# A four-layer image kernel: DVE's product with C one state later, a meter for layer 1's taps, and tiles that rest behind their stores

## The chip, the cores and the metric

The kernel runs on one core of a Trainium2 chip. The metric is the device time of one execution in microseconds. The engines are named as in the profile: PE is TensorE (PEld its weight loads), DVE is VectorE, ACT is ScalarE, POOL is GpSimd, and SP is SyncE, whose queue issues nearly all DMAs of the main part. Each engine works through its own instructions in the order in which the program was written.

## The reference

Four images of 384 channels and 48 x 48 pixels (2304 tokens) pass through four layers. Each layer normalises over groups of channels (`_gn`) and adds its result to its input.

```python
# layer 0, for each image, over 2304 tokens in order (d = 768 channels, s = 16 states)
xin, z = split(gn(x) @ in_proj.T)
xin = silu(causal_depthwise_conv4(xin))
dt, B, C = split(xin @ x_proj.T); dt = softplus(dt @ dt_proj.T + b)
h = exp(dt * A) * h + dt * B * xin        # a scan for each channel and state
y = sum_s(h * C) + xin * D                # the product with C, added over the states
x = x + layer_norm((y * silu(z)) @ out_proj.T)
# layer 1: 1x1 conv, a filter on 8x8 patches in the Fourier domain, a 3x3 depthwise
#          conv (9 taps), gelu(first half) * second half, 1x1 conv
# layer 2: an 11x11 depthwise conv
# layer 3: 4 experts (two 384x384 products with relu), weighted by a top-2 router
```

## The kernel before

**Layer 0 and its slots.** An image is cut into five chunks of 460 or 464 tokens (`CHUNKS`). A chunk has 96 steps, called slots here: 6 blocks of 128 channels times 16 states. So there are 4 x 5 x 96 = 1920 slots (`N`), and `scans` writes the program out slot by slot, in the order in which each engine is to run it. For state `u`, `decay(u)` (line 942, ACT) writes exp(dt A) to a PSUM bank `da`; `drive(u)` (line 953, POOL) writes `bu`, the input times B; `scan(u)` (line 966, DVE) runs the recurrence; the product with C gives `g`; and `turned` (line 886, PE) transposes and adds `g` into `y`. The product runs on POOL in slow slots (`product`, line 995; then the scan writes to `g` in SBUF) and on DVE in the others (`product_now`, line 986; then the scan writes over `da`). In image 0 one slot in three is slow, later every second one. `keep` (line 980, ACT) copies the scan's last column to `carry` for the next chunk; in a slot that is not slow it comes after the product.

There are three banks for `da` in image 0 (the bank for `acc` serves as the third) and two later. Decays are issued three slots ahead in image 0, two ahead later. `bu` has three buffers, `g` six. B and C of a pair of slots come from HBM, broadcast to all partitions, by `spread` (line 930), which issues on SP.

**Everything else.** All other work is cut into tasks, which are Python generators. Each `yield` names a kind of step: "act", "pe", "dve" and "late" (DVE work after the product), "pool", with a weight, a ring of buffers that it needs, and a condition. A task takes at most one step a slot. `Lane.step` goes through the active tasks, and a step runs if its ring has a free buffer. A step with a weight also needs the meter: it counts PE work by weight, falls by 2.3 a slot, takes 0.44 for the slot's own adds, and admits up to 3.7. Steps on DVE have no weight and are not limited, with one exception: layer 1's nine taps of a block (`taps` in `finish_strip`, lines 1413 and 1415) go in threes in slots with `place % 4 < 2`, in twos in the others.

The lanes are `aux` (the rest of layer 0: projections, gates, output projection, layer norm, residual), `start` (during image 0: statistics and z projections of images 2 and 3, kept in HBM), `one` (layers 1, 2 and 3's router of the image before, in this order, begun 42 slots into an image) and `two` (the experts: for each image 4 experts times 16 strips of 144 tokens, 64 blocks). A block loads a strip of x3d (and from the second expert on the partial sum y3d), runs two products on PE (line 1750), adds on DVE (line 1782, or 1785 for the first expert) and stores. What the scans have not taken of image 2's work follows in the tail with image 3's layers; the experts of image 3 end it (`all_experts`, lines 1850 and 1867).

**Rings.** `Ring` counts the buffers of a tile in the planner. A buffer counts as free once `done` was called for it, which for a stored tile is right behind the issue of the store. The hardware still makes the next load into it wait until the store has landed; that wait stands in SP's queue.

Of the kernel before, what the change touches and what calls it, by code (L numbers as in the profile page):

```python
# [16 lines left out]
P = 128  # L17
# [11 lines left out]
NE = 4  # L29
# [13 lines left out]

class Ring:


    def __init__(self, make, n):
        self.make, self.n, self.read = make, n, []

    def free(self, k=1):  # L50
        return all(self.read[: max(0, len(self.read) + k - self.n)])
# [6 lines left out]
    def done(self, k):  # L58
        self.read[k] = True


class Meter:


    def __init__(self, each, limit):
        self.each, self.limit, self.value = each, limit, 0.0

    def slot(self, given):
        self.value = max(0.0, self.value - self.each) + given
# [25 lines left out]
class Lane:  # L95
# [7 lines left out]
    def step(self, phase, slot, at=0):  # L103
        for task in self.active:
            if task.ended:
                continue
            kind, weight, ring, when = task.next
            if PHASE.get(kind, 1) != phase or task.after > slot:
                continue
            if weight and self.bound and self.meter.value + weight > self.meter.limit:  # L110
                continue
            if (ring and not ring[0].free(ring[1])) or (when and not when()):
                continue
            self.meter.value += weight
            task.move(slot)
        self.active = [t for t in self.active if not t.ended]
        while (
            self.queue and len(self.active) < self.width and self.queue[0].at <= max(at, slot)
            and all(t.ended for t in self.queue[0].needs)
        ):  # L120
            task = self.queue.pop(0)
            task.move()
            if not task.ended:
                self.active.append(task)

    def drain(self, slot, others=()):
        n = 0
        while self.queue or self.active:
            self.meter.value = 0.0
            for phase in range(3):  # L130
                for lane in (self, *others):
                    lane.step(phase, slot + n, 1 << 30)
            n += 1
            assert n < 20000, "stuck"
# [8 lines left out]
def tile_layers(ctx: ExitStack, tc: tile.TileContext, a: dict, out: bass.AP):  # L143
# [22 lines left out]
    gexp = const("gexp", [GROUPS, C], a["c_gexp"])  # L166
# [8 lines left out]
    def group_norm(st, bank, mean, rstd, name):  # L175

        mv = small.tile([P, CT, 2], F32, name=f"mv{name}", tag="mv")
        for ct in range(CT):
            nc.vector.bn_aggr(mv[:, ct, :], st[:, ct].rearrange("p k s -> p (k s)"))

        def to_groups(src, n, what):
            ps = bank(f"g{what}{name}")
            for ct in range(CT):
                nc.tensor.matmul(
                    ps[:GROUPS, :n], lhsT=gsel[:, ct, :], rhs=src(ct),
                    start=ct == 0, stop=ct == CT - 1,
                )
            return ps[:GROUPS, :n]

        def to_channels(src, n, what):  # L190
            ps = bank(f"c{what}{name}")
            for ct in range(CT):
                nc.tensor.matmul(
                    ps[:, n * ct : n * ct + n], lhsT=gexp[:, bass.ts(ct, P)], rhs=src,
                    start=True, stop=True,
                )
            return ps[:, : n * CT]

        grp = small.tile([GROUPS, 2], F32, name=f"grp{name}", tag="grp")
        nc.vector.tensor_copy(grp, to_groups(lambda ct: mv[:, ct, :], 2, "m"))  # L200
        nc.vector.tensor_copy(mean, to_channels(grp[:, 0:1], 1, "m"))
        dev = small.tile([P, CT], F32, name=f"dev{name}", tag="dev")
        nc.vector.tensor_sub(dev, mv[:, :, 0], mean)
        nc.vector.tensor_mul(dev, dev, dev)
        var = small.tile([GROUPS, 1], F32, name=f"var{name}", tag="var")
        nc.vector.scalar_tensor_tensor(
            var, to_groups(lambda ct: dev[:, ct : ct + 1], 1, "v"), GN_EPS, grp[:, 1:2],
            ALU.add, ALU.add,
        )
        nc.gpsimd.tensor_tensor(var, var, neghalf[:GROUPS, 0:1], ALU.pow)  # L210
        nc.vector.tensor_copy(rstd, to_channels(var, 1, "v"))

    def group_norm_steps(st, ring, mean, rstd, name):
# [15 lines left out]
        def to_channels(src, n, what):  # L229
            ps, k = ring.take(f"c{what}{name}")  # L230
            for ct in range(CT):
                nc.tensor.matmul(
                    ps[:, n * ct : n * ct + n], lhsT=gexp[:, bass.ts(ct, P)], rhs=src,
                    start=True, stop=True,
                )
            return ps[:, : n * CT], k
# [179 lines left out]
    with ExitStack() as first:  # L416
# [55 lines left out]
        stats0 = wp.tile([P, 2, CT, 2, 3, 6], F32, name="stats0")  # L472
# [86 lines left out]
        def scans(wk, mm, ring, meter, place, lanes, begin):  # L559
# [9 lines left out]
            def image_stats(b, ct, h):  # L569
# [4 lines left out]
                for k in range(3):  # L574
                    yield ("dve",)
                    nc.vector.bn_stats(stats0[:, b % 2, ct, h, k, :], t[:, bass.ts(k, LB)])

            def image_norm(b):
                yield from group_norm_steps(
                    stats0[:, b % 2].rearrange("p c h k s -> p c (h k) s"), ring,  # L580
# [4 lines left out]
            def early_stats(b, ct, h):  # L585
# [6 lines left out]
                for k3 in range(3):  # L592
                    yield ("dve",)
# [9 lines left out]
            def early_fold(b):  # L603
# [21 lines left out]
                yield ("dve",)  # L625
# [11 lines left out]
            def early_z(b, t, j):  # L637
# [22 lines left out]
                yield ("pool",)  # L660
# [28 lines left out]
            def fold(b, which):  # L689
# [22 lines left out]
                yield ("dve",)  # L712
# [25 lines left out]
            def project(i, j):  # L738
# [27 lines left out]
                yield ("dve",)  # L766
# [74 lines left out]
            def steps(i, p):  # L841
# [22 lines left out]
                yield ("dve",)  # L864
# [146 lines left out]
            def gate(i, m):  # L1011
# [9 lines left out]
                yield ("late",)  # L1021
# [4 lines left out]
            def out_proj(i, k):  # L1026
# [20 lines left out]
                yield ("dve",)  # L1047
# [4 lines left out]
            def layer_norm(i):  # L1052
# [8 lines left out]
                yield ("dve",)  # L1061
# [12 lines left out]
            def residual(i, ct):  # L1074
# [14 lines left out]
                yield ("dve",)  # L1089
# [86 lines left out]
            for tag, shape, n in (  # L1176
# [7 lines left out]
                    n,  # L1184
# [14 lines left out]
            with tc.manual_schedule():  # L1199
# [10 lines left out]
                for u in range(N + 6):  # L1210
# [17 lines left out]
                    meter.slot(0.44)  # L1228
                    soon = u % PAIR >= 8
# [5 lines left out]
                    if u < N:  # L1235
# [3 lines left out]
                    if decays < N and decays <= u + (3 if decays < LEN * NC else 2):  # L1239
# [15 lines left out]
                while aux.queue or aux.active:  # L1255
                    at += 1
                    meter.slot(0.0)
                    for phase in range(3):
# [5 lines left out]

        def slow_slot():
            return place[0] % 4 < 2

        def later(b, ring, accr):
# [11 lines left out]
            def slots(tag, shape, n):  # L1280

                return Ring(
                    lambda name: d["wk"].tile(shape, F32, name=name, tag=tag, bufs=n), n
# [11 lines left out]
            def begin1():  # L1295
# [3 lines left out]
                w = d["w_out"] = wk.tile([P, 2, C], F32, name=f"w_out1_{b}", tag="w_out", bufs=1)  # L1299
                nc.sync.dma_start(w[:, 0, :], a["L1_w_outT"][:P, :])  # L1300
                nc.sync.dma_start(w[64:P, 1, :], a["L1_w_outT"][P:, :])
# [38 lines left out]
            def patches(hb, wb):  # L1340
# [24 lines left out]
                yield ("late",)  # L1365
# [27 lines left out]
            def finish_strip(hb):  # L1393
# [7 lines left out]
                def taps(ct):  # L1401
# [3 lines left out]
                    room = 3 if slow_slot() else 2  # L1405
                    for k in range(9):
                        if not room:
                            yield ("dve",)
                            room = 3 if slow_slot() else 2
                        room -= 1  # L1410
# [18 lines left out]
                yield ("dve",)  # L1429
# [6 lines left out]
                yield ("dve",)  # L1436
# [3 lines left out]
                for ct in range(CT):  # L1440
# [3 lines left out]
                        ps[:, :LB], lhsT=w[:, 0, bass.ts(ct, P)], rhs=act[:, 0, :],  # L1444
# [3 lines left out]
                        ps[:, :LB], lhsT=w[64:P, 1, bass.ts(ct, P)], rhs=act[64:P, 1, :],  # L1448
                        start=False, stop=True,
                    )  # L1450
                    yield ("late",)
# [26 lines left out]
            xbs = slots("xb", [P, max(BANDS) * W], 2)  # L1478
# [68 lines left out]
            def windows(ct, k, r, first, last, final):  # L1547
# [26 lines left out]
                if last:  # L1574
                    yield ("late",)
# [5 lines left out]
                    yield ("pool",)  # L1581
# [40 lines left out]
            xg = slots("xg", [P, CT, LB], 2)  # L1622

            def begin3():
# [16 lines left out]
                yield ("dve",)  # L1641
# [4 lines left out]
            def scores_of(hb):  # L1646
# [23 lines left out]
                yield ("dve",)  # L1670
# [17 lines left out]
        def experts(b, ring, rings):  # L1688
# [15 lines left out]
            def begin(e):  # L1704
# [21 lines left out]
                yield ("late",)  # L1726
# [4 lines left out]
            def load3(s, e):  # L1731
                yield (
                    "pool", 0, None,
                    lambda: rings["xe"].free() and (not e or rings["ye"].free()),
                )
                x = take(("x", s, e), "xe", f"xe{b}_{s}_{e}")
                nc.sync.dma_start(x, strip(x3d[b], bass.ts(s, EB)))
                if e:
                    y = take(("y", s, e), "ye", f"ye{b}_{s}_{e}")
                    nc.sync.dma_start(y, strip(y3d, bass.ts(s, EB)))  # L1740
                yield from wait(3)

            def block(s, e):
# [33 lines left out]
                yield ("late",)  # L1777
                key = ("y" if e else "x", s, e)
                x = d[key][0]
                if e:  # L1780
                    y = x.rearrange("p c t -> p (c t)")
                    nc.vector.tensor_add(y, ps[:, : CT * EB], y)  # L1782
                else:
                    for m in range(CT):
                        nc.vector.scalar_tensor_tensor(
                            x[:, m, :], ps[:, bass.ts(m, EB)], b2_sum[:, m : m + 1],
                            x[:, m, :], ALU.add, ALU.add,
                        )
                ring.done(r)
                yield ("pool",)  # L1790
                nc.sync.dma_start(strip(out[b] if e == NE - 1 else y3d, bass.ts(s, EB)), x)
                done(key)
# [106 lines left out]
        def of_experts(pool, sizes):  # L1899
            for tag, n in sizes.items():  # L1900
# [5 lines left out]
                    n,  # L1906
# [11 lines left out]
        meter = Meter(2.3, 3.7)  # L1918
        one, two = Lane(8, meter), Lane(4, meter)

        def begin(b):
# [10 lines left out]
            {"we": 1, "xe": 2, "ye": 2, "hr": 1},  # L1932
        )
        with (
# [7 lines left out]
            while not all(ring.read):  # L1942
# [6 lines left out]
        with (  # L1949
# [4 lines left out]
            of_experts(wk, {"we": 2, "xe": 3, "ye": 3, "hr": 3})  # L1954

            one.queue += later(NB - 1, ring, accr)
            while one.queue or one.active or two.queue or two.active:
                at += 1
                meter.slot(0.0)
                if not (one.queue or one.active):  # L1960
# [124 lines left out]
```

## Time and profile before

| | |
|---|---|
| median of 3 runs | 5400.23 us (5399.6 to 5402.55) |
| the profiled execution | 5405.14 us, span 5403.1 us |
| busy over the span | PE 86%, DVE 75%, POOL 62%, ACT 55% |
| image 0 (480 slots) | 86 to 1047 us |
| images 1, 2, 3 | to 2161, 3344 and 4516 us |
| tail | to 5403 us |
| a scan on DVE | 1.17 us, 1920 times |
| a product with C on DVE, on POOL | 0.63 us, 1035 times; 1.16 us, 885 times |
| a decay on ACT, a `bu` on POOL | 0.65 us, 1.17 us, 1920 times each |
| taps on DVE (line 1415) | 0.615 us, 576 times |
| PE work of the experts in lane `two` | 485.0 + 484.7 us for 192 blocks |

The times of images are those of the first scan of each, counted from the span's start. An engine's busy share is an average over stages in which different engines are scarce, so each stage is read by itself. A row of waits names the instruction that stood idle, and what released it.

### The profile page before, as it was taken

The page shows a single profiled execution, that of the slowest core. Times are in us where ns is not written, and L with a number is a line of the kernel's source. Part 1 is how long each engine was busy: PE and PEld are TensorE (multiplying, and loading weights), DVE is VectorE, ACT ScalarE, POOL GpSimd, SP SyncE. Part 2 cuts the span into 40 slices and gives each one's busy share as a digit, 9 for nine tenths or more (in the row PEclk, how much of TensorE's full clock was granted, in tenths as well). Part 3 has the DMA queues.
Part 4 walks back from the last instruction along what each step waited for, and adds up shares of the span by engine and source line. Part 5 has one row for each costly group of instructions (what it writes and reads, how often), then busy time and mean ns, then how long its engine had stood idle before and what let it go on. Part 6 is the DMA issues. An engine that isn't in the chain of part 4 may idle for free. (4 is left out here: it accounts for less than half of the span.)

```text
span 5403.1 us, 82006 instructions
## 1 busy us (share of the span) xinstructions
PE 4646.1 (86%) x27796; PEld 3666.7 (68%) x27796; DVE 4067.1 (75%) x5581; ACT 2989.0 (55%) x6632; POOL 3363.1 (62%) x3020
## 2 busy tenths in 40 slices
PE   5898877787768988888889988888799988999899
PEld 3555545454446766765668867665678877889799
DVE  5998899889997888889887778798987875452200
ACT  3566655565547765565567745565477653335321
POOL 3788778886677788876678678775677783000000
PEclk8898987788879999998899999998899999999899
DMA  4565545443344555655566565655566573543210
GB/s 152 172 187 175 178 128 150 129 143 120 111 127 131 148 165 157 191 161 147 149 172 178 161 200 155 173 146 149 154 182 174 158 213 115 175 138 105 64 27 23
DMA packets 648873, 794.36 MB, mean 147 GB/s; under 512 B 60149, under 2 KB 642661, under 8 KB 648062
## 3 DMA queue, kind: packets, MB, share of 16 engines
q1 hardware_dynamic: 638148, 787.38, 49.9%
q8 instruction: 221, 3.62, 0.3%
q10 hardware_dynamic: 10298, 1.67, 0.2%
q14 instruction: 206, 1.69, 0.1%
HBM read 685.04 MB, written 103.81 MB: 146 GB/s over the span
## 5 line engine op out<-in xcount | busy, mean ns | idle before, releaser
L953 POOL TENSOR_TENSOR bu<-u,B 128x460 f32<-128x460 f32 (+1 forms) x1920 | 2227.0, 1170 | 795.5 <-DVE g L966 349.8
L942 ACT ACTIVATE da<-dt,a_neg 128x460 f32<-128x460 f32 (+1 forms) x1920 | 1242.4, 648 | 310.6 <-DVE g L986 185.6
L886 PE MATMUL y<-ident,g 128*115 128x128 f32 (+1 forms) x7680 | 1111.3, 292 | 192.5 <-DVE g L986 114.8
L886 PEld LDWEIGHTS y<-ident,g 128*115 128x115 f32 (+1 forms) x7680 | 991.2, 183 | 400.4 <-DVE g L986 140.5
L995 POOL TENSOR_TENSOR g<-g,C 128x460 f32<-128x460 f32 (+1 forms) x885 | 1030.0, 1164 | 246.8 <-ACT carry L980 244.3
L966 DVE TENSOR_TENSOR_SCAN da<-da,carry,bu 128x460 f32<-128x460 f32 (+1 forms) x828 | 971.7, 1174 | 122.2 <-ACT da L942 76.7
L966 DVE TENSOR_TENSOR_SCAN g<-da,carry,bu 128x460 f32<-128x460 f32 (+1 forms) x708 | 819.8, 1167 | 57.7 <-issue 18.8
L986 DVE TENSOR_TENSOR g<-da,C 128x460 f32<-128x460 f32 (+1 forms) x1035 | 656.4, 634 | 175.7 <-DMA C<-bcd 62.0
L980 ACT COPY carry<-da 128x1 f32<-128x1 f32 x828 | 130.3, 157 | 760.5 <-DVE g L986 758.0
L1750 PE MATMUL pout<-hr,we 128*128 128x144 f32 x3456 | 485.0, 297 | 51.5 <-ACT hr L1766 37.8
L1750 PE MATMUL ph<-xe,we 128*128 128x144 f32 x3456 | 484.7, 298 | 33.6 <-DMA xe<-x3d 18.9
L1750 PEld LDWEIGHTS pout<-hr,we 128*128 128x128 f32 x3456 | 456.3, 197 | 75.3 <-ACT hr L1766 47.9
L1750 PEld LDWEIGHTS ph<-xe,we 128*128 128x128 f32 x3456 | 459.4, 199 | 51.5 <-DMA xe<-x3d 13.7
L1557 PE MATMUL pc<-band,row 128*128 128x162 f32 (+14 forms) x3456 | 451.3, 284 | 11.2 <-ACT row L1544 10.9
L1557 PEld LDWEIGHTS pc<-band,row 128*128 128x128 f32 x3456 | 440.0, 194 | 16.6 <-ACT row L1544 11.9
L749 PE MATMUL pin<-xch,w_inx 128*128 128x463 f32 (+2 forms) x720 | 344.8, 621 | 55.1 <-DMA xch<-in_x 32.3
L1415 DVE SCALAR_TENSOR_TENSOR dw<-pad,w_dw,dw 128x384 f32<-128x384 f32 x576 | 348.0, 615 | 20.4 <-ACT pad L1390 9.6
L1037 PE MATMUL po<-w_out,zs 128*115 128x384 f32 (+1 forms) x960 | 342.2, 499 | 14.7 <-DVE ye L1782 9.3
L1766 ACT ACTIVATE hr<-ph,nb 128x144 f32<-128x144 f32 x576 | 176.2, 376 | 279.2 <-PE ph L1750 278.4
L1524 ACT ACTIVATE rep<-x,br,wr 128x192 f32<-128x192 f32 x576 | 273.7, 540 | 4.2 <-issue 4.2
L768 DVE SCALAR_TENSOR_TENSOR xc<-pin,conv_w,xc 128x460 f32<-128x460 f32 (+1 forms) x360 | 249.2, 692 | 30.7 <-ACT xc L762 18.5
L749 PEld LDWEIGHTS pin<-xch,w_inx 128*128 128x128 f32 x720 | 143.8, 213 | 179.8 <-issue 136.3
(211 smaller groups left out, 5979.2 us busy)
## 6 DMA issues: line engine op xcount, KB each, us to landing
B<-bcd SPq DMA_DIRECT2D x768, 230.0 KB, 3.6
C<-bcd SPq DMA_DIRECT2D x768, 230.0 KB, 4.0
B<-bcd SPq DMA_DIRECT2D x192, 232.0 KB, 3.8
C<-bcd SPq DMA_DIRECT2D x192, 232.0 KB, 4.3
xe<-x3d SPq DMA_DIRECT2D x192, 216.0 KB, 2.8
ye<-y3d SPq DMA_DIRECT2D x144, 216.0 KB, 2.8
y3d<-ye SPq DMA_DIRECT2D x96, 216.0 KB, 2.2
xs<-x1d SPq DMA_DIRECT2D x24, 576.0 KB, 5.2
```

What stands on the lines that cost most here:

```text
L749: nc.tensor.matmul(ps[:, lo : halo + n], lhsT=w_inx[:, k, bass.ts(j, P)], rhs=c["x"][:, k, lo : halo + n], start=k == 0, stop=k == CT - 1,)
L886: nc.tensor.matmul(c["y", m][:w, bass.ts(k, P)], lhsT=src[:, bass.ts(k, w)], rhs=ident, is_transpose=True, start=c["terms", m] == 1 and k ...
L942: nc.scalar.activation(da[:, :n], c["dt", p][:, m % 2, :n], AF.Exp, scale=a_neg[:, m, s : s + 1])
L953: nc.gpsimd.tensor_mul(bu[:, :n], c["u", p][:, m % 2, :n], live["B", u // 2][:, :n])
L966: nc.vector.tensor_tensor_scan(here[:, :n], da[:, :n], bu[:, :n], last if t else nil[:, 0:1], ALU.mult, ALU.add,)
L986: nc.vector.tensor_mul(live["g", u][:, :n], live["h", u][:, :n], live["C", u // 2][:, :n])
L995: nc.gpsimd.tensor_mul(g[:, :n], g[:, :n], live["C", u // 2][:, :n])
L1037: nc.tensor.matmul(ps[:w, :C], lhsT=c["zs"][:, m, bass.ts(k, w)], rhs=w_out0[:, m, :], start=m == 0, stop=m == MT - 1,)
L1415: nc.vector.scalar_tensor_tensor(v, src, w_dw[:, ct, k : k + 1], v, ALU.mult, ALU.add)
L1524: nc.scalar.activation(rep[:, :, n, :, :].rearrange("p g r c -> p r g c"), rows.rearrange("p (r g c) -> p r g c", r=BR, c=BC), AF.Identity ...
L1557: nc.tensor.matmul(d["acc2"][0][:, : BANDS[k] * W].rearrange("p (h w) -> p h w", w=W)[:, lo - edges[k] : hi - edges[k], xlo:xhi], lhsT=d[" ...
L1750: nc.tensor.matmul(ps[:, bass.ts(m, EB)], lhsT=w[:, k, bass.ts(m, P)], rhs=of[:, k, :], start=k == 0, stop=k == CT - 1,)
```

## The change

- In image 0 the slot `u` issues the product of state `u - 1` behind the scan of state `u`, and `keep(u - 1)` behind it. Decays are issued at most two slots ahead everywhere.
- A second meter, `meter.vector`, counts DVE work. It falls by 2.4 a slot, not below -1.2, and takes 1.17 in a slow slot and 1.74 in another. All DVE steps now have weights, which only add to it. The taps of layer 1 alone ask it: a tap of weight 0.57 goes if the sum stays within 3.4, else it waits for the next slot.
- Rings get a `rest`: a buffer counts as free so many slots after `done`. It is 2 for the early tiles, `xb` and `ye`, 1 for `xg` and `xe`; for the experts this holds in the scans alone. Stores of z, x3d, y3d and out are issued two slots behind their last step instead of one; the experts' loads wait two slots instead of three.
- `ye` has three buffers in the scans instead of two, `xb` four instead of two. The first expert writes its sum to `ye` too, not over `xe`. Room comes from `stats0` (one image instead of two) and from the second half of layer 1's output weights, which is loaded once into the unused partitions of `gexp`, from ACT's queue, instead of once an image.

```diff
 class Ring:
-    def __init__(self, make, n):
-        self.make, self.n, self.read = make, n, []
+    def __init__(self, make, n, rest=0):
+        self.make, self.n, self.read, self.rest = make, n, [], rest
     def free(self, k=1):
-        return all(self.read[: max(0, len(self.read) + k - self.n)])
+        return all(
+            v is not False and v + self.rest <= CLOCK[0]
+            for v in self.read[: max(0, len(self.read) + k - self.n)]
+        )
     def done(self, k):
-        self.read[k] = True
+        self.read[k] = CLOCK[0]
 class Meter:
-    def __init__(self, each, limit):
-        self.each, self.limit, self.value = each, limit, 0.0
+    def __init__(self, each, limit, least=0.0):
+        self.each, self.limit, self.least, self.value = each, limit, least, 0.0
     def slot(self, given):
-        self.value = max(0.0, self.value - self.each) + given
+        self.value = max(self.least, self.value - self.each) + given
+    def admits(self, weight):
+        return self.value + weight <= self.limit
...
     def step(self, phase, slot, at=0):
+        CLOCK[0] = slot
...
-            if weight and self.bound and self.meter.value + weight > self.meter.limit:
+            meter = self.meter if kind == "pe" else self.meter.vector
+            if kind == "pe" and weight and self.bound and not meter.admits(weight):
                 continue
...
-            self.meter.value += weight
+            meter.value += weight
...
+    gexp = cp.tile([P, C], F32, name="gexp")
+    nc.sync.dma_start(gexp[:GROUPS, :], a["c_gexp"])
+    nc.scalar.dma_start(gexp[64:P, :], a["L1_w_outT"][P:, :])
...
                     meter.slot(0.44)
+                    meter.vector.slot(0.0 if u >= N else 1.17 if where(u)[4] else 1.74)
...
-                    if u < N:
+                    if 0 < u <= LEN * NC:
+                        product_now(u - 1)
+                    if LEN * NC <= u < N:
                         product_now(u)
...
-                    if decays < N and decays <= u + (3 if decays < LEN * NC else 2):
+                    if decays < N and decays <= u + 2:
                         decay(decays)
...
                 def taps(ct):
...
-                    room = 3 if slow_slot() else 2
                     for k in range(9):
-                        if not room:
+                        while not meter.vector.admits(0.57):
                             yield ("dve",)
-                            room = 3 if slow_slot() else 2
-                        room -= 1
+                        meter.vector.value += 0.57
...
-            xbs = slots("xb", [P, max(BANDS) * W], 2)
+            xbs = slots("xb", [P, max(BANDS) * W], 4, 2)
...
-                    yield ("pool",)
+                    yield from wait(2)
                     nc.sync.dma_start(x3d[b][of_band(ct, k)], x[:, :n])
                     xbs.done(xk)
...
             def load3(s, e):
                 yield (
                     "pool", 0, None,
-                    lambda: rings["xe"].free() and (not e or rings["ye"].free()),
+                    lambda: rings["xe"].free() and rings["ye"].free(),
                 )
...
+                y = take(("y", s, e), "ye", f"ye{b}_{s}_{e}")
                 if e:
-                    y = take(("y", s, e), "ye", f"ye{b}_{s}_{e}")
                     nc.sync.dma_start(y, strip(y3d, bass.ts(s, EB)))
-                yield from wait(3)
+                yield from wait(2)
...
+        meter.vector = Meter(2.4, 3.4, -1.2)
...
-            {"we": 1, "xe": 2, "ye": 2, "hr": 1},
+            {"we": 1, "xe": 2, "ye": 3, "hr": 1}, {"xe": 1, "ye": 2},
```

## The prediction

> **What bounds the kernel now.** I first cut the span at the starts of the scans: image 0 runs from 86 to 1047 us, image 1 to 2161, image 2 to 3344, image 3 to 4516; a tail without scans ends at 5403. The view of busy time by stretch (PE, PEld, DVE, ACT, POOL, then clock, DMA share, GB/s) says what is scarce in each:
>
> ```profile
> 86.00:1047.00 961.00, 773.60 (x3441) 509.07 (x3442) 868.11 (x1092) 572.39 (x1188) 776.08 (x689) 0.87 0.55 164
> 2161.00:3344.00 1183.00, 1045.31 (x6634) 852.28 (x6635) 993.02 (x1339) 718.55 (x1617) 860.61 (x771) 0.94 0.58 168
> 2380.00:2653.00 273.00, 223.15 (x1143) 165.05 (x1143) 247.48 (x354) 149.95 (x336) 173.11 (x157) 0.87 0.49 144
> 3125.00:3344.00 219.00, 193.17 (x1232) 154.60 (x1232) 172.64 (x230) 113.75 (x208) 170.97 (x153) 0.95 0.61 178
> 4516.00:5403.00 887.00, 835.87 (x6122) 771.40 (x6122) 228.20 (x498) 282.10 (x718) 4.25 (x14) 0.96 0.31 89
> ```
>
> Image 0 is DVE's: 868 of 961 us, 2.00 us for each of its 480 slots (a slot is one state's scan). Image 2 alternates. Its second chunk of 96 slots (2380 to 2653), where layer 1's taps run, is DVE's, at 2.84 us a slot; its last (3125 to 3344), mostly experts, takes 2.28 us and neither DVE (79%) nor PE (88%) is full. The tail is PE's, 94%. So time is won by closing DVE's gaps in image 0, by levelling DVE in images 1 to 3, and by stalls that idle both; work pushed into the tail is paid there.
>
> The second view is the order in time in image 0 (start, duration):
>
> ```profile
> 599.55 1.17 DVE L966 TENSOR_TENSOR_SCAN da<-da,carry,bu 128x460 f32<-128x460 f32 x1
> ...
> 600.83 0.64 DVE L986 TENSOR_TENSOR g<-da,C 128x460 f32<-128x460 f32 x1
> ...
> 601.38 1.17 DVE L966 TENSOR_TENSOR_SCAN g<-da,carry,bu 128x460 f32<-128x460 f32 x1
> 601.50 0.16 ACT L980 COPY carry<-da 128x1 f32<-128x1 f32 x1 [0.34 <-DVE g L986]
> 601.69 0.65 ACT L942 ACTIVATE da<-dt,a_neg 128x460 f32<-128x460 f32 x1
> ```
>
> The product that reads its own scan's output starts 0.11 us after the scan ends; the next scan, which needs nothing of it, starts 0.09 us before the product ends. ACT's copy of the carry waits for the product, and the next decay into the freed bank stands behind that copy.
>
> The third view is who waits for whom in image 2, of DVE and then of SP's queue (total us, times, longest):
>
> ```profile
> DVE da L966 <- ACT da L942: 34.2, 24, 6.1
> DVE g L986 <- DMA C<-bcd: 21.8, 11, 5.8
> ```
>
> ```profile
> SPq L1740 <- DMA y3d<-ye: 98.4, 32, 7.5
> SPq L1791 <- DVE ye L1782: 71.4, 25, 7.6
> SPq L1737 <- DMA y3d<-xe: 59.4, 15, 6.6
> SPq L1740 <- DMA out<-ye: 54.5, 14, 7.2
> SPq L1513 <- DMA x3d<-xb: 43.3, 13, 5.4
> ```
>
> SP is one queue in order. Each load into a tile whose store is still under way, and each store whose sum is not ready, holds the B and C loads of the scan behind it.
>
> **The product behind the next scan (image 0).** Over all direct neighbours in image 0, 253 products behind their own scan start 0.098 us late on average, and 291 scans behind a product start 0.072 us early. After the move both kinds are free neighbours, so a pair gains 0.170 us: 253 x 0.170 = 43 us. The Trainium skill speaks against it: "VectorE: DVE Perf Modes", section "The DRAIN you can't avoid", says the next op does not start until the pipe is empty and that chaining without semaphores is no faster, which would make the gain 0. The rows show -0.08 against +0.09 us, so I take the row.
>
> The price: a product now ends one scan later, and decay(u+2) must follow it, through the bank and behind the carry copy. Counting from scan(3k), which is slow, with net steps of 1.09 (scan) and 0.55 (product): product(3k-1) ends at 1.72, carry and decay end near 2.6, scan(3k+2) is due at 2.73. Slack is 0.1 us in one slot of three; the same count before gives about 1.9. So any ACT work that runs past the product delays a scan. ACT's other work in image 0 is about 200 us (572 less 310 of decays and 64 of carries). Bounds: 0 if DVE's other work covers it, 66 if a third of those 200 us is exposed. The nearest rows are images 1 to 3, where decays run two slots ahead: DVE's waits for da there are 32, 40 and 35 us. I take 30. What is late next is POOL: three bu and one product per three slots are 4 x 1.17 = 4.7 us against DVE's 4.4 without side work; that is inside the 30. Net **-13** (-43 to +23).
>
> **Layer 1's taps by a meter.** Nothing is removed: 162 taps an image, 0.615 us each. They move in time. Before, two or three went in each slot. Now a slot gives 2.4 and takes on average 1.455 for scan and product, 0.26 for layer 0 (25.0 of weights per 96 slots), about 0.09 for experts. That leaves 0.60, or 0.69 in image 1 without experts. A strip weighs 27 x 0.57 for taps plus 5.57 for its other DVE steps, 21.0: so 35 slots a strip, 31 in image 1. The stores of x2d stand 24 slots apart now. Layer 1 grows by about 68 slots in images 2 and 3 and 40 in image 1.
>
> Image 2 by slots: layer 1's 142 at 2.84 plus 68 of the experts' kind at 2.28 are 558 us. After, 210 slots at a budget of 2.4: 504 if DVE never idles, 554 at the 91% busy of the row (247/273). I take 93%, near the row: 2.58 x 210 = 542, -16. The same in image 3; image 1 gives 472 to 469. Sum **-35** (-110 to 0).
>
> The cost comes at the end. Layer 3 of image 2 closes at slot 1855 now; 68 later is past the last slot, 1919. The nine blocks of image 2's experts that start inside the scans today (134 of 192 blocks are before the last scan) move to the tail at 5.0 us of PE each (485.0 and 484.7 us of PE over 192): +45. The slots they leave were 89% PE (178.6 of 201 us), so about 20 returns: **+25** (0 to +110, the latter if a slower layer 1 displaces more).
>
> **Tiles rest behind their stores.** Loads wait out two slots (4.6 us) against landings of 2.2 us for y3d and 4.5 us for out in the list of DMA issues; stores step back one slot. The five SP rows above, 327 us in image 2, should nearly vanish. Only what reaches the engines counts. DVE's waits for DMA in images 1 to 3 are 7 + 22 + 31 = 60 us; POOL's for B in images 2 and 3 are 54 + 37 = 90, of which DVE's own waits for bu, 12 + 11 + 8, are the visible part. Part is covered where PE is the limit. Bounds 0 and -90, **-45** taken.
>
> **The rest, at nothing.** A third ye lets blocks follow every 3.3 slots instead of the 4 seen in stretches with experts alone, but only 64 blocks an image exist; cover gone, it is worth up to -25. Early z tasks go from about 3.75 to 4.75 slots each (60 of them, slots 61 to 286): they end near 350, before the drain at 480; if not, the rest drains at once. The extra gexp load costs ACT's queue 0.4 us, hidden by its idle from 25.5 to 29.5 us at the start. The missing w_out load saves SP 0.4 us an image. Two more xb tiles lengthen no step of the windows' chain. The first expert writes y instead of x, at the same three operations.
>
> **Sum:** -13 - 35 + 25 - 45 = -68 us. The profiled execution took 5405.1 us with a span of 5403.1; the median of the runs is 5400.2, 4.9 less. 5405.1 - 68 - 4.9 gives about **5332**. About 0.2%, 11 us, is what a measurement can tell from no change.
>
> **Rivals.** *Layer 1 too slow* (slower than before; chance 0.16): the meter starves taps until layer 1 takes some 240 slots, and layer 3 overruns the next image's begin at slot 42. Each slot of delay then costs expert blocks, at one per 4 slots and 5.0 us. It decides from about 14 more blocks in the tail (68/5.0). At 20 more, 5332 + 100 = 5432. For it: the budget leaves taps only 0.6 us a slot. Against: bursts of six are allowed, and experts have some 450 slots for 64 blocks.
>
> *Everything was hidden* (0.13): PE, 88% busy in images 2 and 3, takes over as stalls go, and da waits eat image 0's gain: -10 to 0, about 5395.
>
> *Both engines fill* (0.16): the 504 end of the meter's sum (-35 becomes -110) with 60 instead of 45 of the stalls: 5332 - 90 = 5242; halfway, 5287.
>
> The likeliest, -68, has 0.55, with its own range 5290 to 5375. Faster: 0.55 + 0.16 + part of the hidden case = 0.74; same 0.07; slower 0.19. The range 5260 to 5420 leaves out some 0.08 below and 0.12 above.
>
> **What would show it.** Image 0: products start 0.08 us before the scan ahead of them ends, its length falls from 961 to about 948, and DVE's waits for da rise from 9 to about 30 us. Images 1 to 3: taps over some 200 slots instead of 135, their chunk below 2.7 us a slot; SP's waits at L1740 and L1791 near zero; C waits gone. Tail: from 887 to about 930 us. I am wrong if image 0 grows (ACT's loop binds), if the tail grows by over 100 us, or if C waits persist.

## The result and the profile after

The changed kernel takes 5321.24 us (5315.81 to 5325.88, 4 runs) beside 5399.91 us before; the ratio is 0.9856, 95% interval 0.9839 to 0.9873, which is 79 us less. The forecast was 5332 us, in a range of 5260 to 5420. The profiled execution has a span of 5316.4 us. By stage, from first scan to first scan, this is where the time went:

| stage | before | after | difference | foretold |
|---|---|---|---|---|
| image 0 | 960.1 | 951.4 | -9 | -13 |
| image 1 | 1114.0 | 1102.7 | -11 | -3 and some stalls |
| image 2 | 1183.6 | 1146.9 | -37 | -16 and about -20 of stalls |
| image 3 | 1172.2 | 1126.4 | -46 | the same, -20 more for blocks that leave |
| tail | 886.7 | 902.3 | +16 | +45 |

The view of busy time by stretch of the changed kernel (length; PE, PEld, DVE, ACT, POOL busy; clock; DMA share; GB/s):

```profile
87.00:1038.00 951.00, 779.77 (x3440) 508.62 (x3440) 846.63 (x1090) 568.77 (x1188) 771.03 (x687) 0.88 0.55 165
...
2141.00:3288.00 1147.00, 1036.11 (x6677) 859.38 (x6678) 993.65 (x1342) 718.59 (x1619) 864.40 (x774) 0.94 0.59 172
...
2357.00:2593.00 236.00, 214.60 (x1308) 173.48 (x1307) 216.96 (x306) 145.22 (x338) 170.30 (x155) 0.95 0.60 176
...
4414.00:5316.00 902.00, 867.92 (x6416) 798.26 (x6416) 234.61 (x523) 291.56 (x744) 4.64 (x15) 0.98 0.32 94
```

Image 2 holds the same DVE work as before (994 against 993 us) in 37 us less. Its second chunk now takes 2.46 us a slot instead of 2.84, with DVE at 92% and PE at 91%: both engines are nearly full in the same stretch, where before PE stood at 82%. The tail has 32 us more of PE work, and only 16 us more of time, as its PE idles 34 us instead of 51.

The order in time on DVE in image 0 of the changed kernel:

```profile
601.03 0.62 DVE L1001 TENSOR_TENSOR g<-da,C 128x460 f32<-128x460 f32 x1
601.57 1.17 DVE L981 TENSOR_TENSOR_SCAN g<-da,carry,bu 128x460 f32<-128x460 f32 x1
602.64 2.14 DVE L783 SCALAR_TENSOR_TENSOR xc<-pin,conv_w,xc 128x460 f32<-128x460 f32 x3
```

Each instruction starts before the one ahead of it has ended: 601.03 + 0.62 is 601.65, and the scan starts at 601.57. All 221 products directly behind a scan in image 0 start early, by 0.089 us on average; before, the 253 of them started 0.098 us late. The gain is there, and so is its price, in the waits of DVE in image 0 (total us, times, longest), first before:

```profile
DVE da L966 <- ACT carry L980: 14.7, 3, 5.1
DVE da L966 <- ACT da L942: 8.8, 2, 4.5
```

and in the changed kernel:

```profile
DVE da L981 <- ACT da L957: 32.4, 31, 4.0
DVE g L981 <- issue: 31.6, 7, 6.5
```

The five stops of before are one in each chunk, of 4.3 to 5.1 us, while ACT runs its two silu passes of a chunk (2.50 and 2.49 us) and loads tables around them (1.28 us each), so that no decay comes. In the changed kernel the same five stops stand in the row "issue", at 5.7 to 6.5 us each. The 31 waits for da are new and short. Of SP's waits in image 2, these are the largest at the experts' loads and stores (L1752 loads xe, L1755 loads ye, L1806 stores):

```profile
SPq L1752 <- PE ph L1765: 44.0, 16, 8.7
SPq L1752 <- DVE ye L1799: 43.2, 12, 7.9
SPq L1755 <- DMA y3d<-ye: 28.6, 12, 5.6
...
SPq L1806 <- DVE ye L1796: 19.6, 12, 3.3
...
SPq L1755 <- DMA out<-ye: 8.8, 4, 3.4
```

The last three were 98, 71 and 55 us. They fell as foretold, though not to near zero, and the loads of xe took over a part: their waits of all kinds rose from 72 to 98 us, while those of ye's loads fell from 154 to 37 and those of the stores from 101 to 25. DVE's wait for C in images 2 and 3 fell from 52.3 to 1.6 us, as foretold. Whether the rests are also what saved the time is the point that the experiments had to decide.

### The profile page after: what moved, and what is told of

Its sections match the earlier page's. It is cut to its first block, busy times and chain, and to the rows that moved or that the text cites. A ratio compares the mean times of both kernels' runs of the same rounds, so it can differ in the third digit from the quotient of the medians.

```text
span 5316.4 us, 82000 instructions
## 1 busy us (share of the span) xinstructions
PE 4608.1 (87%) x27796; PEld 3649.6 (69%) x27796; DVE 4033.3 (76%) x5581; ACT 2987.1 (56%) x6632; POOL 3360.1 (63%) x3020
## 5 line engine op out<-in xcount | busy, mean ns | idle before, releaser
L764 PE MATMUL pin<-xch,w_inx 128*128 128x463 f32 (+2 forms) x720 | 322.3, 586 | 12.2 <-DMA xch<-in_x 7.5
L981 DVE TENSOR_TENSOR_SCAN da<-da,nil,bu 128x460 f32<-128x460 f32 x207 | 241.3, 1173 | 32.2 <-ACT carry L995 20.7
```

What stands on the lines that cost most here:

```text
L764: nc.tensor.matmul(ps[:, lo : halo + n], lhsT=w_inx[:, k, bass.ts(j, P)], rhs=c["x"][:, k, lo : halo + n], start=k == 0, stop=k == CT - 1,)
L981: nc.vector.tensor_tensor_scan(here[:, :n], da[:, :n], bu[:, :n], last if t else nil[:, 0:1], ALU.mult, ALU.add,)
```

## The experiments

Each ratio is to the kernel before, run beside it on the same chip. "Blocks" are the experts' blocks, of 192, whose second product is done before the last scan ends. The stages are in us and from one profile each; the row "before" stems from an execution of 5405 us, while beside the other runs that kernel took 5412 to 5415, so small differences of stages to it say little.

| run | product's move | meter | buffers | rests | ratio, 95% interval | blocks | images 1 to 3 | tail |
|---|---|---|---|---|---|---|---|---|
| before | | | | | 1 | 134 | 3470 | 887 |
| the change | x | x | x | x | 0.9856 (0.9839 to 0.9873) | 128 | 3376 | 902 |
| order_alone | x | | | | 0.9969 (0.9959 to 0.9979) | 134 | 3468 | 887 |
| meter_alone | | x | | | 0.9917 (0.9903 to 0.9931) | 128 | 3418 | 906 |
| rest_alone | | | x | x | 0.9888 (0.9873 to 0.9903) | 140 | 3452 | 843 |
| rings_only | | | x | | 0.9844 (0.983 to 0.9857) | 143 | 3432 | 842 |
| ye_only | | | ye alone | | 0.9862 (0.9847 to 0.9877) | 143 | 3448 | 841 |
| no_order | | x | x | x | 0.9852 (0.9838 to 0.9865) | 128 | 3372 | 902 |
| no_meter | x | | x | x | 0.9867 (0.9852 to 0.9882) | 140 | 3448 | 842 |
| meter_rings | x | x | x | | 0.9864 (0.9848 to 0.9879) | 128 | 3401 | 894 |
| order_rings | x | | x | | 0.9825 (0.9812 to 0.9838) | 143 | 3429 | 841 |
| experts_rest | x | | x | experts' | 0.983 (0.9812 to 0.9848) | 140 | 3444 | 840 |
| budget27 | x | at 2.7 | x | x | 0.9899 (0.9884 to 0.9915) | 132 | 3452 | 874 |
| keep_first | x, copy first | x | x | x | 0.9895 (0.988 to 0.991) | 128 | 3376 | 902 |

One part of the change is hidden in the column "buffers": every run with buffers also has the experts' loads waiting two slots instead of three. No run took the two apart. (All runs but order_alone also keep the moved load of layer 1's output weights.) With 128 blocks, all of images 0 and 1 are done and none of image 2.

**One part alone.** Three kernels take one part of the change each. My theory was the prediction's sum; the rivals were that levelling DVE is the main gain, and that the stalls had been hidden by PE. Their cores:

```diff
# order_alone: on the kernel before
-                    if u < N:
+                    if 0 < u <= LEN * NC:
+                        product_now(u - 1)
+                    if LEN * NC <= u < N:
                         product_now(u)
...
-                    if decays < N and decays <= u + (3 if decays < LEN * NC else 2):
+                    if decays < N and decays <= u + 2:
# meter_alone: on the kernel before
...
-                        if not room:
+                        while not meter.vector.admits(0.57):
                             yield ("dve",)
...
# rest_alone: on the kernel before; all rests, later stores, added buffers, loads' shorter wait
...
-            {"we": 1, "xe": 2, "ye": 2, "hr": 1},
+            {"we": 1, "xe": 2, "ye": 3, "hr": 1}, {"xe": 1, "ye": 2},
...
-            xbs = slots("xb", [P, max(BANDS) * W], 2)
+            xbs = slots("xb", [P, max(BANDS) * W], 4, 2)
```

> Only the product behind the next scan in image 0, with decays two slots ahead. By the prediction's sum (43 us of gaps closed, 30 given back as waits for da): -13 us, about 5387; the change's image 0 got shorter by 9, so 5391. If the moved product has nothing to do with image 0's 9 us (rival: the early tasks' rests did it), 5400 or more. Image 0: waits for da about 30 us.

> Only the meter of DVE for layer 1's taps; rings, stores and image 0 as before. By the prediction's sum: -35 in images 1 to 3, +25 in the tail, about 5390. Rival, that levelling DVE is the main gain: -60 or more, below 5340, with B and C waits still there.

> Only the rests, the later stores and the added buffers; taps and image 0 as before. By the prediction's sum: -45 us, about 5355, images 2 and 3 shorter by some 20 each, DVE's waits for C near zero, tail about as before. Rival, that the stalls were hidden by PE: -15 to 0, 5385 to 5400.

The product's move alone gave 0.31%, some 17 us, where 13 were foretold. In the seven profiles with the move (keep_first aside) image 0 takes 949.8 to 958.0 us, in the six without it 959.8 to 967.4: 12 us less on average. The meter alone gave 0.83%, 45 us, where 10 were expected and the rival asked for 60: images 1 to 3 lost 52 us and the tail gained 20. The rests' part, which holds the buffers and the loads' shorter wait too, gave 1.12%, 61 us, but not where it was expected. Images 2 and 3 are 11 us shorter in sum, and 44 us are gone from the tail, although the stalls have vanished. In image 2 of rest_alone DVE waits for C only this long:

```profile
DVE g L1001 <- DMA C<-bcd: 1.0, 1, 1.0
```

Six more blocks fit before the last scan, at some 5 us of PE each, which is most of what the tail lost. So the parts meet in one place: the meter takes blocks out of the scans (134 to 128), something in the rests' part puts them in (134 to 140). If their gains were free of each other, the three would give 0.9775; the change gives 0.9856.

**Two parts together.** I took one part out of the whole.

```diff
# no_meter: on the changed kernel
...
-                        while not meter.vector.admits(0.57):
+                        if not room:
                             yield ("dve",)
...
# no_order: on the changed kernel
-                    if 0 < u <= LEN * NC:
-                        product_now(u - 1)
-                    if LEN * NC <= u < N:
+                    if u < N:
                         product_now(u)
...
-                    if decays < N and decays <= u + 2:
+                    if decays < N and decays <= u + (3 if decays < LEN * NC else 2):
```

> The change without the meter: product order and rests, layer 1's taps in twos and threes as before. If the meter and the rests add up, the meter's own gain of 0.8% is missing: ratio about 0.994, worse than the change's 0.9856. If the meter takes back in the tail what the rests win there (140 blocks before the last scan with rests alone, 128 in the change), the meter is worth little on top of them: ratio 0.986 (0.9969 x 0.9888), tail about 845 us, image 3 about 1155.

> The change without the product's move: meter and rests. If the parts added up: ratio 0.981 (0.9917 x 0.9888), better than the change. If meter and rests draw on the same gain and the move is worth 0.3% here too: ratio 0.988 to 0.989, image 0 about 964 us, tail about 902.

Without the meter the change measures 0.9867, its interval across the change's own: on top of the rests' part the meter is worth nothing that can be told. Images 1 to 3 are 72 us longer, the tail 60 us shorter. Without the product's move the ratio is 0.9852, neither the 0.981 of free gains nor a loss that shows; image 0 is 967.4 us there against 951.4, but the totals do not differ. That the move is worth its 0.3% in the company of both others was not shown.

**A faster meter.**

```diff
# budget27: on the changed kernel
-        meter.vector = Meter(2.4, 3.4, -1.2)
+        meter.vector = Meter(2.7, 3.4, -1.2)
```

> The whole change with 2.7 instead of 2.4 a slot in DVE's meter. By the weights, taps then get 0.9 us a slot and a strip takes some 23 to 25 slots, near the 24 of before; layer 3 of image 2 closes near slot 1850 and 10 or more blocks of its experts fit before the last scan. If the tail's growth is this delay, the tail falls from 902 to 845-870 while images 1 to 3 grow by 15 to 40 in all: total 5290 to 5320, ratio 0.981 to 0.985. Rival, that the level of DVE is what counts: images 1 to 3 grow by more than the tail gives, ratio above 0.987.

The ratio is 0.9899 (0.9884 to 0.9915), worse than with 2.4 and worse than without a meter. Layer 3 of image 2 has its first product on PE at slot 1874 instead of 1917 and its last at 1890, four blocks fit before the last scan where ten or more were expected, and the tail shrinks to 874 us, but images 1 to 3 grow by 76 us to 3452. The rival was right: what the tail gets back is less than the lost level costs. Why 2.7 is worse in image 1 (1130 us) than the old twos and threes (1114) was not settled.

**Buffers or rests.** In rest_alone several things change together. This kernel keeps the buffers and drops the rests and later stores, those of the early tiles, z, xg and x3d too; the experts' loads still wait two slots instead of three:

```diff
# rings_only: on rest_alone
...
-            xbs = slots("xb", [P, max(BANDS) * W], 4, 2)
+            xbs = slots("xb", [P, max(BANDS) * W], 4)
...
-            {"we": 1, "xe": 2, "ye": 3, "hr": 1}, {"xe": 1, "ye": 2},
+            {"we": 1, "xe": 2, "ye": 3, "hr": 1}, {},
...
                 ring.done(r)
-                yield from wait(2)
+                yield ("pool",)
                 nc.sync.dma_start(strip(out[b] if e == NE - 1 else y3d, bass.ts(s, EB)), y)
```

> Of the rests' part only the added buffers (three ye, four xb, the first expert's sum in ye), with no rest and stores one slot behind as before. If the gain of that part is SP's queue freed of waits on stores, little is left: ratio 0.996 to 1.001, DVE's waits for C as before. If it is that a third ye lets blocks follow faster, most of it stays: ratio 0.989 to 0.992, 138 or more blocks before the last scan, tail about 845 to 860.

This decided against my step. The ratio is 0.9844: the buffers and the shorter wait give more without the rests than with them (0.9888), and by themselves as much as the whole change. Image 2 and the tail of rings_only by stretch:

```profile
2169.00:3342.00 1173.00, 1062.91 (x6816) 872.69 (x6815) 1000.37 (x1355) 722.03 (x1633) 862.22 (x772) 0.95 0.59 171
...
4485.00:5327.00 842.00, 793.14 (x5798) 727.09 (x5798) 219.85 (x470) 274.11 (x691) 4.26 (x14) 0.96 0.30 88
```

Image 2 takes 10 us less than before and holds 18 us more PE work; the tail has 43 us of PE work less, which is nine blocks at 5 us. The scans of images 1 to 3 are 38 us shorter besides. Of these, 27 lie in the last two chunks of image 3 (236 and 202 us before, 225 and 186 now); what shortens them was not settled. SP's queue still stands at the experts' tiles in image 2, though less than before:

```profile
SPq L1809 <- DVE ye L1799: 93.2, 30, 6.5
...
SPq L1758 <- DMA y3d<-ye: 36.8, 17, 5.3
SPq L1809 <- DVE ye L1802: 32.7, 15, 4.3
```

Without any rest most waits of a load on a store are gone already (98 to 37 us), and the waits of stores on their sums (126 us in these two rows) do no harm that shows.

```diff
# ye_only: on rings_only
-            xbs = slots("xb", [P, max(BANDS) * W], 4)
+            xbs = slots("xb", [P, max(BANDS) * W], 2)
```

> Of the added buffers only the third ye (with the first expert's sum in it); xb stays at two. If ye carries the gain: ratio 0.983 to 0.987 and 140 or more blocks before the last scan. If xb does: 0.992 or more, with SP's waits of xb loads on x3d stores (43 us in image 2) back.

0.9862, and all 143 blocks are there, so the gain does not hang on xb: the two more xb are worth at most the 0.2% to 0.9844, and the intervals overlap. The stalls can be a small part of it at most, as DVE still waits 41.4 us for C and POOL 72.5 us for B in images 2 and 3 (52.3 and 90.5 before). How the blocks come in can be read in the slots. Before, layer 3 of image 2 is through at slot 1857, but the experts are busy with image 1 until slot 1885, and the first block of image 2 starts at 1894. In ye_only image 1's blocks end at slot 1828 and those of image 2 start at 1864, so 15 of them are done instead of 6.

What lets the blocks follow faster is not settled, because ye_only keeps the loads' shorter wait. The order in which the kernels are written out, which needs no run on the chip, has 134 blocks ahead of the last scan before and 143 in ye_only, as the profiles do. With the third ye alone it has 139, with the shorter wait alone 141. Either can therefore bring blocks in; what each is worth in time was not measured.

**Buffers with the other parts.**

> The product's move and the added buffers, without meter, rests and later stores. If both gains are free of each other: ratio 0.981 (0.9969 x 0.9844), about 28 us below the change, with 143 blocks before the last scan and a tail near 842 us. If the gains overlap: 0.984 to 0.986, no better than the change.

> The change without rests and later stores: product's move, meter and added buffers. If rests and later stores only cost (0.9888 with them, 0.9844 without, taps as before), this is faster than the change too: ratio 0.979 to 0.984. If the rests pay once taps are levelled, because images 2 and 3 then have no other slack: 0.986 or more, with DVE's and POOL's waits for DMA back at 60 us and over in images 2 and 3.

order_rings is no_meter without rests and later stores, meter_rings the change without them (the edit is that of rings_only). order_rings measures 0.9825 and is, with experts_rest (0.983), the fastest kernel of the study; by the intervals it lies just under the change, which did not run beside it. meter_rings measures 0.9864, so beside the buffers the meter costs: images 1 to 3 fall by 28 us (3429 to 3401) and the tail grows by 53 (841 to 894), as 15 blocks move behind the last scan. With the meter, rests or no rests makes no difference that can be told (0.9856 and 0.9864).

**Which rests cost.**

```diff
# experts_rest: on order_rings, the rests and later stores of the experts put back
...
-            {"we": 1, "xe": 2, "ye": 3, "hr": 1}, {},
+            {"we": 1, "xe": 2, "ye": 3, "hr": 1}, {"xe": 1, "ye": 2},
...
-                yield ("pool",)
+                yield from wait(2)
                 nc.sync.dma_start(strip(out[b] if e == NE - 1 else y3d, bass.ts(s, EB)), y)
```

> The product's move, the added buffers, and of the rests and later stores only those of the experts (xe, ye, their stores); those of the early tiles, of xb, of x3d's stores and of xg are undone, and taps go as before. Without any rests this measured 0.9825, with all of them 0.9867. If the cost of the rests is the longer chain of layers 2 and 3 (layer 3 of image 0 closed at slot 900 instead of 886, which moves the experts' start): 0.979 to 0.983, layer 3 back at 886, C waits near zero. If it is the experts' own longer hold on ye, which pushes blocks out: 0.985 to 0.988, 139 to 141 blocks before the last scan.

0.983, the same as order_rings. This is the nearest test of the stalls. These are DVE's waits for C and POOL's for B in images 2 and 3 of order_rings, then of experts_rest:

```profile
DVE g L1001 <- DMA C<-bcd: 31.3, 12, 6.4
POOL bu L968 <- DMA B<-bcd: 54.4, 20, 5.2
```

```profile
DVE g L1001 <- DMA C<-bcd: 4.8, 2, 4.5
POOL bu L968 <- DMA B<-bcd: 10.7, 8, 3.3
```

They fall by 26 and 44 us, and the time doesn't move. It is a net, as three blocks fall behind the last scan (143 to 140); clearing the stalls with the blocks held at 143 was not tried. With all rests (no_meter) it is 0.9867, and the intervals are apart, so the other rests cost some 20 us. They are those of xb, xg and the early tiles, with the later stores of x3d and z; with them layer 3 of image 0 has its first product at slot 900 instead of 886 (this is the event that the expectation calls "closed"), and the experts start 16 slots later. That the delay is what costs was not tried by itself, and it costs no blocks: 140 are done in both.

**ACT's copy ahead of the product.** This one tests the price of the move in image 0.

```diff
# keep_first: on the changed kernel
...
+                    if 0 < u <= LEN * NC and not where(u - 1)[4]:
+                        keep(u - 1, False)
                     if u < N:
                         scan(u)
...
-                        product_now(u - 1)
+                        product_now(u - 1, True)
```

> The whole change, but in image 0 ACT copies the carry out of the bank during the next scan, ahead of the product on DVE, so a decay waits for the product alone and not for product and copy. If image 0's missing 30 us are ACT's short slack (0.1 us in one slot of three), 0.19 us more slack takes half or more of the waits for da away: image 0 from 951 to 930-942, total 5300 to 5312. Rival, that the lost time is POOL's or the long silu stops: image 0 stays at 948 to 953, total 5321.

It went the other way: 0.9895 (0.988 to 0.991), image 0 999.7 us instead of 951.4. The waits for da are gone, as wished; another wait came in their place:

```profile
DVE g L1001 <- ACT carry L995: 123.2, 81, 6.4
```

The order in time shows how:

```profile
600.75 0.15 ACT L995 COPY carry<-da 128x1 f32<-128x1 f32 x1
...
600.93 0.64 DVE L1001 TENSOR_TENSOR g<-da,C 128x460 f32<-128x460 f32 x1
```

Both only read the bank, yet the second waits for the first, whichever engine it is on. Here DVE waits whenever ACT is late with a copy of 0.15 us; before and in the change it is ACT that waits. The short slack is real, but this cure puts ACT's queue on DVE's path 81 times.

## Why the prediction was right, and where it was not

**The sum** was -68 us, and 79 came. Two of its steps met their marks in mechanism; a third, the rests, was given a gain that the rests do not bring, and among the things costed at nothing stands a gain as large as the whole change's. That the total came out near is in that part luck.

**The product behind the next scan** (-43 and +30, net -13): right. Neighbours went from +0.098 to -0.089 us, da waits from 9 to 32 us, image 0 fell by 9, and alone the move gave 17. The row was the right choice, but the Trainium skill does not stand against it: in "VectorE: DVE Perf Modes", the section "The DRAIN you can't avoid" also says that a next op that is not held starts earlier, which is what all 221 products do (-0.089 us). What was not foretold is that decays two slots ahead lengthen the stop at ACT's silus from 4.3-5.1 to 5.7-6.5 us in each of the five chunks, about 8 us in all.

**Layer 1 by slots**: right. A strip was worked out at 31 and 35 slots, layer 1 at 186 and 210; it ran over slots 565 to 752, 1046 to 1260 and 1526 to 1737. Layer 3 of image 2 has its first product at slot 1917, where it was 1837 before: 80 slots later, of which the rests make 14 (1851 in rest_alone); 68 were foretold for its end, which now lies behind the last scan. The slot's length was taken at 2.58 us and came out at 2.49 over layer 1, so the term of -35 was too small: alone the meter took 52 us from images 1 to 3.

**The tail** (+45, of which 20 return): the mechanism right, the size too large. I counted nine blocks of image 2 that begin before the last scan; the first products say seven, and six are done (134 to 128). PE's work in the tail grew by 32 us and the time by 16.

**"Tiles rest behind their stores", -45**: this step failed. DVE's and POOL's waits vanished as foretold, but experts_rest clears them and gains nothing, rings_only and order_rings leave about half of them in place and are as fast or faster than the change, and ye_only leaves four fifths and gains 75 us. I took DVE's and POOL's idle before a late B or C as time on the path. Of the bounds that I gave, 0 and -90, what the rests bring is the first, net of the blocks that they delay.

**"The rest, at nothing"**: here stood the third ye, with "only 64 blocks an image exist" as the reason and -25 as the end. Together with the loads' shorter wait, for which the prediction has no term at all, it measures 0.9862, 75 us. The reason was wrong, because the number of blocks an image is not the limit; how many are done when the last scan ends is, and blocks that follow sooner bring each later image's experts forward too (143 instead of 134). Nine blocks explain the 46 us of the tail, not the 22 by which images 1 to 3 are shorter in ye_only. My tail step priced exactly this, at 5.0 us a block, and I did not apply it to the buffers.

**The rivals.** "Layer 1 too slow" did not come to pass, yet its mechanism is the meter's true cost: with the buffers, the meter moves 15 blocks and 53 us into the tail for 28 us won. "Everything was hidden" was right for the stalls alone.

## What to carry to other kernels

Before pricing a stall, ask what runs out at the end of the stage it is in; here the time hung on how much of one lane's work was done when another lane ended, and a third buffer with a shorter wait of the loads moved that, while removed waits did not. Test buffers and delays apart when a change brings both: the delays were no help to the buffers, and those outside the experts cost about 20 us. Look in each trial for what it keeps besides: here a wait of one slot less stayed in every run with buffers and was not told from them. Two parts that each win may be trading the same work back and forth, so the one to keep is found by taking each out of the whole.

## What was not expected of the hardware

A DVE instruction that needs nothing of the one ahead starts 0.07 to 0.09 us before that one's recorded end, one that needs its result 0.09 to 0.10 us after it; over the pairs of scan and product in image 0 the difference, about 0.18 us, is more than a quarter of a product. And two engines that only read the same PSUM bank stand one behind the other in this program in both orders: the copy waits for the product (173.9 us of ACT's idle time in image 0 of the change), or the product for the copy (123.2 us of DVE's in keep_first). These waits are written into the program; whether the chip needs them, no run here shows.
